# Projecting nodes for layer 1 of a four-layer graph attention stack while layer 0 still gathers

## The chip, the cores and the metric

The kernel runs on one core of one Trainium2 chip. The metric is device time in microseconds (us), the median of several executions. A profile of one execution is read beside it. The engines are called TensorE (PE in the profile, PEld for its weight loads), VectorE (DVE), ScalarE (ACT), GpSimd (POOL) and SyncE (SP). Transfers are issued by an engine's queue and moved by 16 DMA engines.

## The reference

There are 3327 nodes with 256 features and an adjacency matrix in which a node has some 32 neighbours, itself among them. Four attention layers follow one another. Each ends in a residual sum and a layer normalisation over the features.

```python
x = layernorm(x + gatv2(x, adj, ...))   # layer 0
x = layernorm(x + gat(x, adj, ...))     # layer 1
x = layernorm(x + linear_att(x, adj))   # layer 2
x = layernorm(x + two_gat_layers(x))    # layer 3, 4 heads, twice

# layer 0: score[i,j] = sum_c a[c] * leaky_relu(g_src[i,c] + g_tgt[j,c])
# layer 1: Wh = h @ W.T ; s1 = Wh @ a1 ; s2 = Wh @ a2
#          e = leaky_relu(s1[:,None] + s2[None,:]) ; masked by adj
#          out = softmax(e, axis=1) @ Wh
# layer 2: as layer 1 without leaky_relu, with a bias
# layer 3: as layer 1 with 4 heads of 64 features and elu, applied twice
```

In layer 0 the score doesn't split into a part of i and a part of j, so it is worked out only for the neighbours. In the other layers the exponential of the score does split, up to a maximum of two terms, and the sum over neighbours becomes a dense matrix product with the adjacency.

## The kernel before

The nodes lie in 26 tiles of 128 rows (the last has 127); h holds the current features of a tile in SBUF through all layers.

*Layer 0* (`sparse0`). The 26 tiles form three groups (`SETS = (5, 9, 12)`). For each tile VectorE extracts the list of neighbours from the adjacency, and nodes of a group are sorted by their number of neighbours. GpSimd then gathers the neighbours' rows from a table in DRAM, up to 8 neighbours of 128 nodes in one step (`parts`; each neighbour is one indirect transfer, L527). VectorE scores them (L546, L552), ScalarE scales rows by their weights (L633) and TensorE adds them up through an identity matrix (L636). The work is written out by step: gathers run four steps ahead (`LEAD`), and a table `due` says which other work is emitted at which step, through `at_step`. Eleven gather buffers (`TURNS`) rotate. When a group's last tile is done, its sums are scattered back to the nodes' order in DRAM (L671), read into h (`take`), and normed (`finish_sums`, `finish_root`, `finish`: L696 to L714). For the last group this comes after all gathers.

*Layers 1 to 3* (`layers`). The target nodes are cut into four blocks of 7, 7, 6 and 6 tiles. For a block, a loop over the 26 source tiles j loads the adjacency tile (`adjacent`; in layer 1 the int32 original, cast to bf16 and stored in DRAM for later layers), makes the edge weights (`weigh`, L1075, VectorE: the larger of the target's rate and the source's, times adjacency), and multiplies them with the source's projected features `feat[j]` (L1159 for one head, L1198 and L1206 for four). After the loop the block's sums are added to h, and a generator `prepare` norms the block and projects it for the next layer: per tile a transpose on TensorE (`turn`, L1104), a copy by ScalarE (L1107), the projection (L1011), and exponentials and scaling by ScalarE (L1018 to L1023). Generators wait in `pending`; `work_off` advances one by a step after each source tile, so that next layer's projection lies between this layer's products. The rates of a block (`rates_of`) are separate products of the transposed features with `w_src` (L1048), their exponential (L1053), a write of the row to DRAM (L1057) and a load that spreads it to all partitions (L1064), both issued by SyncE. For layer 1 all four blocks are prepared ahead of the loop, with weights loaded and their dot products formed at that place. In layer 3's first half, `finish_hidden` does the elu on a block and projects it for the second half, in stages that `staged` spaces by steps.

Where an engine is in a `manual_schedule`, its instructions keep the order of the program; otherwise the framework orders them. In layer 0 all but SyncE are manual; in layers 1 and 2 only TensorE; in layer 3 TensorE, VectorE and ScalarE.

Of the kernel before, what the change touches and what calls it, by code (L numbers as in the profile page):

```python
# [19 lines left out]
P = 128  # L20
# [26 lines left out]
def gat_stack(  # L47
# [55 lines left out]

    def copy_rows(engine, dst, src):

        rows = dst.shape[0]
        whole = rows // 16 * 16
        for lo, hi in ((0, whole), (whole, rows)):
            if lo < hi:
                engine.dma_start(dst[lo:hi], src[lo:hi])  # L110
# [7 lines left out]
    def load_row(work, src, name):  # L118

        size = src.shape[0]  # L120
        t = work.tile([P, size], F32, tag="row_" + name, name=name, bufs=1)
        nc.sync.dma_start(
            t, bass.AP(tensor=src.tensor, offset=src.offset, ap=[[0, P], [1, size]])
        )
        return t
# [124 lines left out]
    def sparse0(lost):  # L250
        GROUP, TURNS, LEAD = 8, 11, 4
        starts = [sum(SETS[:s]) for s in range(len(SETS))]
        with ExitStack() as s0:
# [21 lines left out]
            for c in range(kc):  # L275
                t = io0.tile([P, dim], F32, tag="hs", name="dots0")
# [230 lines left out]
            ]  # L507
            held = {}
# [4 lines left out]
            def gather(q):  # L513
# [11 lines left out]
                g = gath.tile([P, GROUP, ROW], F32, tag=f"g{q % TURNS}", name="g")  # L525
# [86 lines left out]
            def combine(s, t):  # L612
# [30 lines left out]
                for g, k0, m in groups[-1:] + groups[:-1]:  # L643
# [4 lines left out]
                    for k in reversed(range(0, m - 1, 2)):  # L648
# [38 lines left out]
            def finish_sums(s):  # L687

# [4 lines left out]
                for k, it in enumerate(block):  # L693
# [3 lines left out]
                    nc.vector.bn_aggr(mv[:pn, k, :], stats[:pn])  # L697
                rstd = small.tile([P, max(SETS)], F32, tag="rstd0", name="rstd0", bufs=2)
# [10 lines left out]
            def finish(s):  # L709
                mv, rstd = moments.pop(s)  # L710
                for k in range(SETS[s]):
# [5 lines left out]
                    )  # L717

# [25 lines left out]
            for q, key in ends.items():  # L744
                at_step(q + 4, add_input, *key)
                at_step(q + 6, between.append, lambda key=key: put_back(*key))
                if key[1] == SETS[key[0]] - 1:
# [3 lines left out]
                    at_step(q + 18, finish, key[0])  # L751
            for it in range(SETS[0]):
                write_list(0, it)
# [35 lines left out]
            assert not between  # L789

# [182 lines left out]
    def layers(rs):  # L973
# [16 lines left out]
        class Layer:  # L990


            def __init__(self, name, slot, nh, leaky, load, bias=None):
                self.slot, self.nh, self.leaky, self.bias = slot, nh, leaky, bias
                self.weight = work.tile([P, kc, dim + nh], F32, tag="weight", name=name + "w")
                row_src, row_dst = load(self.weight)
                dots(work, self.weight[:, :, dim : dim + nh], self.weight, row_dst, nh)
                if leaky:
                    self.w_src = work.tile([P, kc, nh], F32, tag="w_src", name="w_src")
                    dots(work, self.w_src, self.weight, row_src, nh)  # L1000
                    self.rate_d = dram.tile([heads, n], F32, name=f"rate_{slot}{nh}_d")
# [3 lines left out]
            def project(self, j, ht, banks):  # L1005
# [4 lines left out]
                for k in range(kc):  # L1010
                    nc.tensor.matmul(  # L1011
                        pacc[:pn, : dim + nh], ht[:, k, :pn], self.weight[:, k, :],
# [3 lines left out]
                if self.leaky:  # L1016
# [5 lines left out]
                    for lo in range(0, dim, width):  # L1022
# [3 lines left out]
                        )  # L1026
                else:
# [12 lines left out]
            def rates_of(self, b, ht, banks):  # L1040


                c0, c1 = cols_of(blocks[b])
                for lo in range(0, c1 - c0, BANK):
                    hi = min(lo + BANK, c1 - c0)
                    pr = misc(banks)
                    for k in range(kc):
                        nc.tensor.matmul(  # L1048
                            pr[: self.nh, : hi - lo], self.w_src[:, k, :], ht[:, k, lo:hi],
                            start=(k == 0), stop=(k == kc - 1),  # L1050
                        )
                    row = work.tile([heads, BANK], F32, tag="spread", name="rate_row", bufs=4)
                    nc.scalar.activation(  # L1053
                        row[: self.nh, : hi - lo], pr[: self.nh, : hi - lo], AF.Exp,
                        scale=1.0 - SLOPE,
                    )
                    nc.sync.dma_start(  # L1057
                        self.rate_d[: self.nh, c0 + lo : c0 + hi], row[: self.nh, : hi - lo]
                    )
# [4 lines left out]
                nc.sync.dma_start(  # L1064
# [31 lines left out]
        def turn(b, banks):  # L1096

            ht = turn_p.tile([P, kc, wide], F32, tag="ht", name="ht")
            for it in blocks[b]:
                pn = rows_of(it)  # L1100
                at0 = (it - blocks[b][0]) * P
                tp = misc(banks)
                for k in range(kc):
                    nc.tensor.transpose(  # L1104
                        tp[:, k * P : k * P + pn], h[it][:pn, k * P : (k + 1) * P], ident[:pn, :pn]
                    )
                nc.scalar.copy(  # L1107
                    ht[:, :, at0 : at0 + pn],
                    tp[:, : kc * P].rearrange("p (k i) -> p k i", k=kc)[:, :, :pn],
                )  # L1110
                yield ht, it

        def prepare(nxt, b, banks, normed=True):
# [3 lines left out]
            for ht, it in turn(b, banks):  # L1117
                at0 = (it - blocks[b][0]) * P
                yield
                nxt.project(it, ht[:, :, at0 : at0 + P], banks)  # L1120
                yield
            if nxt.leaky:
                nxt.rates_of(b, ht, banks)
# [19 lines left out]
        def one_head(layer, nxt, banks_next):  # L1143

            for b, block in enumerate(blocks):
                work_until(lambda: not layer.leaky or layer.rate[b] is not None)
                accs = [bank(s) for s in range(len(block))]
                for j in range(nt):
# [17 lines left out]
                    if j >= LATER:  # L1166
                        work_off()
                work_until(lambda: not pending)
                for s, it in enumerate(block):
# [6 lines left out]
                    )  # L1176
                pending.append(prepare(nxt, b, banks_next, normed=False))
# [325 lines left out]
```

The softmax here doesn't subtract the row's maximum and nothing guards it: scores larger than these inputs give would overflow.

## Time and profile before

The median of three executions is 3262.66 us (3262.03 to 3264.55). The profiled execution spans 3261.5 us. Busy time by engine over the span:

| engine | busy us | share |
|---|---|---|
| TensorE | 2224.4 | 68% |
| TensorE weight loads | 1218.1 | 37% |
| VectorE | 2318.1 | 71% |
| ScalarE | 741.5 | 23% |
| GpSimd | 1029.6 | 32% |

Where the stages lie in the span:

| stage | from, to (us) |
|---|---|
| layer 0, until the last tile's weights | 0 to 1523 |
| layer 1's first edge weight | 1593 |
| layer 1, end of blocks 0, 1, 2, 3 | 1706, 1793, 1868, 1943 |
| layer 2 | 1943 to 2228 |
| layer 3, first and second half | 2228 to 2747, 2747 to 3262 |

The shares of the whole span are means over stages with different limits: GpSimd is idle after layer 0, and TensorE is less than half busy in it. So a row of the span says little about what a change in one stage is worth, and the stages are read one by one. Busy time of TensorE is modelled at its ends.

### The profile page before, as it was taken

What the parts mean: (1) busy time and instruction counts of PE and PEld (TensorE: products, weight loads), DVE (VectorE), ACT (ScalarE), POOL (GpSimd) and SP (SyncE); (2) the same over time, 40 slices, a digit from 0 to 9 for tenths busy, and PEclk for the clock granted to TensorE, in tenths of its full rate; (3) what the DMA queues carried; (4) which work ended last, traced back from release to release, by engine and by line L of the source; (5) the groups of instructions that cost most, each with busy time, mean ns of one, the idle gap of its engine ahead of it and who ended that gap; (6) DMA issues with size and microseconds to landing.
All of it is one profiled execution on the core that took longest, in us unless ns stands there. A gap on an engine that the chain in (4) does not pass through costs nothing.

```text
span 3261.5 us, 44647 instructions
## 1 busy us (share of the span) xinstructions
PE 2224.4 (68%) x15644; PEld 1218.1 (37%) x15644; DVE 2318.1 (71%) x6589; ACT 741.5 (23%) x2002; POOL 1029.6 (32%) x1034
## 2 busy tenths in 40 slices
PE   3203332343441444343899999999999999999997
PEld 2101111121220221111478888774334444334342
DVE  6789999999975655554235642117888788899998
ACT  0003231342341343333334431110111110110110
POOL 0077657777767777774000000000000000000000
PEclk7556666666765776676699999999999999999998
DMA  7466536555435444443466753332212212212111
GB/s 216 137 141 180 169 100 150 173 157 155 112 86 109 124 111 113 113 113 91 125 199 199 201 161 93 100 99 72 63 44 68 61 46 65 63 49 57 56 47 48
DMA packets 176842, 364.21 MB, mean 112 GB/s; under 512 B 33746, under 2 KB 118964, under 8 KB 176610
## 3 DMA queue, kind: packets, MB, share of 16 engines
q1 hardware_dynamic: 96682, 183.56, 19.8%
q0 software_dynamic: 49632, 141.57, 16.9%
q10 hardware_dynamic: 30296, 36.15, 3.2%
q8 instruction: 126, 2.06, 0.3%
q14 instruction: 106, 0.87, 0.1%
HBM read 320.99 MB, written 43.58 MB: 112 GB/s over the span
## 4 chain that ended last, share of the span: by engine, by line
PE 46%; DVE 4%; DMA 2%; ACT 1%; issue 1%; DVEq 0%; SPq 0%; POOL 0%; ACTq 0%; POOLq 0%
PE acc L1198 17%; PE acc L1159 15%; PE acc L1206 8%; PE misc L1011 3%; DVE e L1075 3%; PE misc L1048 1%; DMA at_i<-in_adj_t_dram 1%; PE misc L1104 1%; DMA at<-at_d 1%; PE misc L1280 0%; PE misc L1241 0%; PE acc L636 0%; DVE stats L1355 0%; DVE h L1353 0%; ACT feat L1023 0%
## 5 line engine op out<-in xcount | busy, mean ns | idle before, releaser
L527 POOL DMA_INDIRECT g<-table_d,lst x923 | 912.6, 989 | 295.6 <-issue 268.8
L1075 DVE SCALAR_TENSOR_TENSOR e<-rate,feat,at 128x896 f32<-128x896 f32 (+4 forms) x832 | 843.1, 1078 | 67.7 <-PE acc L1206 58.4
L636 PE MATMUL acc<-g,ident 128*128 128x512 f32 (+1 forms) x934 | 454.7, 644 | 545.2 <-ACT g L633 512.7
L1198 PE MATMUL acc<-e,feat 128*32 128x384 f32 (+2 forms) x6656 | 722.8, 514 | 5.2 <-DVE e L1075 2.4
L225 POOL TENSOR_TENSOR rstds<-rstds,minus_half 128x7 f32<-128x7 f32 (+1 forms) x12 | 19.6, 1633 | 1671.7 <-DVE rstds L224 1671.7
L636 PEld LDWEIGHTS acc<-g,ident 128*128 128x128 f32 x934 | 193.3, 211 | 783.7 <-ACT g L633 561.6
L546 DVE TENSOR_TENSOR y<-g,both 128x1024 f32<-128x1024 f32 (+2 forms) x240 | 276.0, 1173 | 238.4 <-DMA g<-table_d,lst 223.5
L1206 PE MATMUL acc<-e,feat 128*32 128x384 f32 (+3 forms) x3328 | 397.5, 512 | 0.0
L1198 PEld LDWEIGHTS acc<-e,feat 128*32 128x32 f32 x6656 | 245.1, 109 | 381.8 <-issue 262.5
L633 ACT ACTIVATE g<-g,w 128x256 f32<-128x256 f32 x923 | 370.6, 494 | 0.0
L552 DVE SCALAR_TENSOR_TENSOR y<-y,both 128x256 f32<-128x256 f32 x923 | 324.5, 415 | 0.0
L1159 PE MATMUL acc<-feat,e 128*128 128x257 f32 (+2 forms) x1352 | 307.4, 381 | 0.6 <-DVE h L1173 0.6
L1159 PEld LDWEIGHTS acc<-feat,e 128*128 128x128 f32 (+2 forms) x1352 | 253.2, 190 | 39.7 <-issue 4.1
L1159 PE MATMUL acc<-feat,at 128*128 128x257 bf16 (+2 forms) x2028 | 240.9, 276 | 7.5 <-DMA at<-at_d 7.3
L466 PE MATMUL key_rows<-key_diag,ones 128*128 128x128 f32 x52 | 17.8, 440 | 314.5 <-DVE key_diag L465 259.5
L1159 PEld LDWEIGHTS <-at 128*128 128x128 bf16 (+2 forms) x2028 | 200.2, 100 | 43.9 <-DMA at<-at_d 8.0
L1075 DVE SCALAR_TENSOR_TENSOR e<-rate,feat,at_i 128x896 f32<-128x896 f32 (+2 forms) x104 | 112.2, 1081 | 143.1 <-DMA at_i<-in_adj_t_dram 109.8
L1206 PEld LDWEIGHTS acc<-e,feat 128*32 128x32 f32 (+1 forms) x3328 | 136.1, 110 | 164.2 <-issue 150.4
L421 DVE MAX8 cand<-num 128x8 f32<-128x64 uint16 x1352 | 178.9, 209 | 1.0
L542 ACT COPY both<-own_of 128x256 f32<-128x256 f32 x26 | 9.7, 374 | 602.1 <-DMA own_of<-own_d,lst 469.2
L466 PEld LDWEIGHTS key_rows<-key_diag,ones 128*128 128x128 f32 x52 | 12.1, 278 | 327.8 <-DVE key_diag L465 216.0
L1092 ACT CAST at<-at_i 128x896 bf16<-128x896 int32 (+2 forms) x104 | 92.0, 885 | 108.5 <-DMA at_i<-in_adj_t_dram 104.2
(158 smaller groups left out, 1707.5 us busy)
## 6 DMA issues: line engine op xcount, KB each, us to landing
at<-at_d SPq DMA_DIRECT2D x150, 224.0 KB
at_i<-in_adj_t_dram SPq DMA_DIRECT2D x50, 448.0 KB
adj_i<-in_adj_dram SPq DMA_DIRECT2D x25, 832.0 KB
adj_i<-in_adj_dram SPq DMA_DIRECT2D x25, 831.5 KB
g<-table_d,lst POOLq DMA_INDIRECT x923, 2.8
at<-at_d SPq DMA_DIRECT2D x75, 192.0 KB
at<-at_d SPq DMA_DIRECT2D x75, 191.8 KB
at_d<-at ACTq DMA_DIRECT2D x50, 224.0 KB
```

The costliest lines, as they stand in the source:

```text
L421: nc.vector.max(cand[:, lo // CHUNK + c, :], v[:, c * CHUNK : (c + 1) * CHUNK])
L527: nc.gpsimd.indirect_dma_start(out=g[:, k - k0, :], out_offset=None, in_=table_d[:, :], in_offset=bass.IndirectOffsetOnAxis(ap=entry["lst" ...
L546: nc.vector.tensor_tensor(y, rows, minus_src[:, None, :].to_broadcast([P, m, dim]), op=ALU.max)
L552: nc.vector.scalar_tensor_tensor(y, y, 1.0, a, op0=ALU.mult, op1=ALU.mult, accum_out=sc)
L633: nc.scalar.activation(rows, rows, AF.Copy, scale=w[:, k : k + 1])
L636: nc.tensor.matmul(dst, ident, rows, start=start, stop=stop)
L1011: nc.tensor.matmul(pacc[:pn, : dim + nh], ht[:, k, :pn], self.weight[:, k, :], start=(k == 0), stop=(k == kc - 1),)
L1075: nc.vector.scalar_tensor_tensor(e[:pn, : c1 - c0], self.rate[b][:pn, h_of, : c1 - c0], q, at[:pn, : c1 - c0], op0=ALU.max, op1=ALU.mult,)
L1092: nc.scalar.copy(at[:pn, :w], at_i[:pn, :w])
L1159: nc.tensor.matmul(accs[s][:pn, : dim + 1], a[:pj, s * P : s * P + pn], f[:pj, : dim + 1], start=(j == 0 and part == 0), stop=(j == nt - 1 ...
L1198: nc.tensor.matmul(accs[x][p][q : q + 32, : hi - lo], f[:pj, at0 : at0 + 32], es[at0 // hd][:pj, lo:hi], start=(j == 0), stop=(j == nt - 1),)
L1206: nc.tensor.matmul(accs[x][pairs][h_of * 32 : (h_of + 1) * 32, : hi - lo], f[:pj, dim + h_of : dim + h_of + 1].to_broadcast([pj, 32]), es[ ...
```

## The change

There are five parts.

1. The first two groups (14 tiles, the first two blocks of layer 1) are transposed and projected for layer 1 at steps of layer 0's last group (`turn_next`, `project_next`), in PSUM that the neighbour lists no longer use. The features go to DRAM (`feats_d`), and so do the rates (`rate1_d`). Layer 1's weights are loaded and their dots formed some steps earlier (`load_next`, `dots_next`) into a tile of their own, `w1`.
2. The last group's reading, moments and norms become a generator, `last_group`, that is worked off between the steps of layer 1's block 0, followed by the projection of the 12 tiles left. `fetch` brings the stored features three tiles ahead. In this block two generator steps are taken at each source tile from the eleventh on, and VectorE, ScalarE, GpSimd and SyncE keep program order.
3. Rates come from the projection: it has as many more columns as heads, their exponential is taken with the features', and each tile's rates are written to DRAM as single elements by ScalarE's queue. `rates_of` only loads them, also on ScalarE's queue. The separate products L1048 are gone, in all layers.
4. In `finish_hidden` elu and projection come at lags 6 and 7 in place of 4 and 5.
5. Smaller: the buffers that gathers rotate through are shifted so that the last ones lie at given places, the last tile's pairs are added in ascending order, layer 2's weights are loaded after layer 1's block 0, and transposed tiles have two small buffers in place of one for a whole block.

```diff
-                g = gath.tile([P, GROUP, ROW], F32, tag=f"g{q % TURNS}", name="g")
+                g = gath.tile([P, GROUP, ROW], F32, tag=f"g{(q + SHIFT) % TURNS}", name="g")
...
+            def turn_next(it):
+                bank = turned1["bank"]
+                for k in range(kc):
+                    nc.tensor.transpose(
+                        bank[:, k * P : (k + 1) * P], h[it][:, k * P : (k + 1) * P], ident
+                    )
+                ht = turned1[it] = io0.tile([P, kc, P], F32, tag="xt", name="ht1", bufs=4)
+                nc.scalar.copy(ht, bank[:, : kc * P].rearrange("p (k i) -> p k i", k=kc))
+
+            def project_next(it):
+                ht, p = turned1.pop(it), turned1["bank"][:, BANK : BANK + dim + 2]
+                project(p, ht, P, w1)
...
+                nc.sync.dma_start(feats_d[at0 : at0 + P, :], f[:, : dim + 2])
+                nc.sync.dma_start(
+                    rate1_d[:, at0 : at0 + P].rearrange("h p -> p h"), f[:, dim + 2 : dim + 3]
+                )
...
-                if key[1] == SETS[key[0]] - 1:
+                if key[1] == SETS[key[0]] - 1 and key[0] < len(SETS) - 1:
                     at_step(q + 10, take, key[0])
...
+            at = begins[len(SETS) - 1]
+            at_step(at - 6, load_next)
+            at_step(at - 3, dots_next, 0)
+            at_step(at - 2, dots_next, 1)
+            for s in range(len(SETS) - 1):
+                for it in range(starts[s], starts[s] + SETS[s]):
+                    at_step(at, turn_next, it)
+                    at_step(at + 2, project_next, it)
+                    at += 3
+                at = max(at, begins[len(SETS) - 1] + 19)
...
+            def last_group():
+                s = len(SETS) - 1
+                take(s)
+                for _ in range(4):
+                    yield
+                yield from settle(s)
+                finish_root(s)
+                yield
+                for lo in range(0, SETS[s], 6):
+                    finish(s, lo, lo + 6)
+                    yield
...
-                        pacc[:pn, : dim + nh], ht[:, k, :pn], self.weight[:, k, :],
+                        pacc[:pn, : dim + self.extra], ht[:, k, :pn], self.weight[:, k, :],
...
+                    rate = small.tile([P, heads], F32, tag="rate", name="rate_of")
+                    nc.scalar.activation(
+                        rate[:pn, :nh], pacc[:pn, dim + nh : dim + 2 * nh], AF.Exp,
+                        scale=1.0 - SLOPE,
+                    )
+                    copy_rows(
+                        nc.scalar,
+                        self.rate_d[:nh, j * P : j * P + pn].rearrange("h p -> p h"),
+                        rate[:pn, :nh],
+                    )
...
-                for lo in range(0, c1 - c0, BANK):
-                    hi = min(lo + BANK, c1 - c0)
-                    pr = misc(banks)
-                    for k in range(kc):
-                        nc.tensor.matmul(
-                            pr[: self.nh, : hi - lo], self.w_src[:, k, :], ht[:, k, lo:hi],
...
-                nc.sync.dma_start(
+                nc.scalar.dma_start(
                     rate[:, : self.nh, : c1 - c0], rows[None].to_broadcast([P, self.nh, c1 - c0])
                 )
...
-                    if j >= LATER:
+                    if layer is l1 and b == 0:
+                        work_off(2 if j > 10 else 1)
+                        fetch([j + 3])
+                        if j > early and late:
+                            l1.rates_of(late.pop(0))
+                    elif j >= LATER:
                         work_off()
                 work_until(lambda: not pending)
+                in_order.close()
...
-            yield from staged(units, [(0, spread), (3, scale), (4, elu), (5, project)])
-            l3b.rates_of(b, o, (6, 7))
+            yield from staged(units, [(0, spread), (3, scale), (6, elu), (7, project)])
+            yield
+            l3b.rates_of(b)
...
-        for b in range(len(blocks)):
-            pending.append(prepare(l1, b, (7,)))
-        work_until(lambda: l1.rate[0] is not None and not pending)
...
+        if early:
+            l1.rates_of(late.pop(0))
+        fetch(range(3))
+        if rest is not None:
+            pending.insert(0, rest)
```

## The prediction

> **What bounds the kernel now.** I read the 40 slices and the busy table of the page first, then the chain that ended last, then busy time by stage, then who waited for whom inside the stages that the change touches, and the timeline where one wait had to be understood.
>
> The table by stage (window, length, busy time and count of each engine, granted TensorE clock, DMA share, GB/s) cuts the span at events of the timeline: last combine of layer 0 at 1523, first layer 1 accumulation at 1598, end of layer 1's block 0 at 1706, end of layer 1 at 1945, layer 3 from 2228.
>
> ```profile
> 167.00:1523.00 1356.00, 498.17 (x1080) 232.45 (x1080) 1062.16 (x4434) 399.95 (x1024) 990.34 (x998) 0.67 0.49 131
> 1523.00:1598.00 75.00, 48.08 (x95) 21.11 (x96) 18.32 (x57) 23.11 (x69) 3.27 (x2) 0.59 0.27 82
> 1598.00:1706.00 108.00, 106.16 (x475) 82.79 (x475) 33.99 (x38) 46.32 (x102) 0.00 (x0) 0.99 0.64 190
> 1706.00:1945.00 239.00, 238.42 (x1120) 207.71 (x1119) 131.65 (x266) 93.62 (x174) 4.27 (x3) 1.00 0.67 194
> 1945.00:2228.00 283.00, 272.20 (x2219) 225.35 (x2217) 49.70 (x176) 43.38 (x176) 5.60 (x4) 0.98 0.35 99
> 2228.00:2747.00 519.00, 515.93 (x5340) 214.50 (x5341) 439.27 (x462) 64.31 (x226) 2.09 (x1) 1.00 0.21 57
> ```
>
> Layer 0 is paced by GpSimd: 923 gathers of 0.95 us with 0.30 us between them, while TensorE, VectorE and ScalarE have room. From 1598 on TensorE is busy nearly all the time. In between lie 75 us where no engine is full and the clock is at 0.59. The waits of 1545 to 1598 say why; the first lines are (who waited, on what: total, times, longest):
>
> ```profile
> DVE e L1075 <- DMA rate<-rate_f_d: 28.0, 1, 28.0
> ACT feat L1018 <- PE misc L1011: 27.7, 9, 10.4
> ...
> PE misc L1011 <- DMA l2w<-in_l_w_dram: 10.6, 1, 10.6
> ```
>
> and the timeline shows one tile's projection as a serial loop through one PSUM bank, 4.0 us from 1568.00 to 1572.00:
>
> ```profile
> 1568.00 0.69 PE L1104 MATMUL misc<-ident,h 128*128 128x128 f32 x2 [0.77 <-ACT feat L1023]
> 1568.72 0.37 ACT L1107 COPY ht<-misc 128x256 f32<-128x256 f32 x1 [0.78 <-PE misc L1104]
> 1569.15 2.08 PE L1011 MATMUL misc<-l1w,ht 128*128 128x257 f32 x4 [0.46 <-ACT ht L1107]
> 1571.27 0.17 ACT L1018 ACTIVATE feat<-misc 128x1 f32<-128x1 f32 x1 [2.17 <-PE misc L1011]
> ```
>
> So layer 1 starts late because weights, seven projections and the rates of block 0 stand in a row ahead of the first edge weight (1593). Block 0 then takes 108 us, as the other projections sit between its steps.
>
> Two smaller items. TensorE's waits in 2016 to 2228 and VectorE's in 2360 to 2880:
>
> ```profile
> PE acc L1159 <- DMA at<-at_d: 7.3, 3, 2.8
> PE misc L1048 <- ACT rate_row L1053: 2.0, 3, 0.7
> ```
>
> ```profile
> DVE o L1299 <- ACT spreads L1258: 42.6, 10, 5.5
> ```
>
> **What the skill says.** "DMA: Bandwidth & Descriptors", section "Queues, rings and completion order", says that each DMA engine goes round between the queues that have work, a packet at a time. The trace agrees with its other half: an adjacency load issued on SyncE at 2083.80, behind the 1792 KB rate load issued on the same queue at 2081.89, reached TensorE only at 2090.14. Its table of specifications says that pieces under 512 B are written by read-modify-write; no row here shows 4-byte pieces, which the change brings. "TensorE: Matmul & The Clock Gate", section "What's actually happening", has the clock halve after an idle window of some 3.4 us; here a 128x257 projection takes 2.08 us in 1545 to 1598 (clock 0.50) and 1.03 at 1619. "Perfetto Trace Analysis", section "Tensor Engine Instruction (MATMUL, LD_WEIGHTS)", calls the execution FIFOs of ScalarE, VectorE and GpSimd strict, unlike that of TensorE; so a ScalarE instruction that waits for TensorE holds all behind it, which the 42.6 us show.
>
> **The change part by part.**
>
> *Projection during layer 0.* 14 of 26 tiles get transposes and projection at one tile in three gather steps. A step is up to 8 gathers at 1.25 us, 10 us. A tile costs, at the slow clock, 0.69+2.08 us of TensorE and 0.37+3x0.17+0.47=1.35 us of ScalarE, in 30 us of which TensorE is busy 37% and ScalarE 29% (stage row). Weight dots add 8 VectorE operations of 0.4 us. GpSimd waited only 6.1 us in all for ScalarE to free a gathered buffer, so I cost this at nothing; it hides behind the gathers.
>
> *Start of block 0.* VectorE's order puts layer 0's last sum (L664, ends 1541.5) ahead of the first edge weight. The first adjacency tile may share memory with the last gathered rows: before, it was issued at 1540.51, its cast began at 1543.95; plus 1.15 us for L1075 gives 1545.1. Were it loaded earlier, 1542.6. I take 1545 for the start, against 1598.
>
> *Length of block 0.* 79 matmuls took 17.28 us at 1783, 0.219 each; 26 steps x 14 = 79.6 us. From the beats of block 1 (1736.20 to 1743.35 holds 28 matmuls, 6.12, and one tile), transposes and projection take 1.03 us on TensorE: 12 tiles, 12.4. In this block two generator steps run per accumulation step from step 11, so transposes and projection stand next to each other and TensorE waits for ScalarE's copy, 0.37 us plus two hand-overs, about 0.6: 12x0.6=7.2. The in-order ScalarE queue holds 13 reads of the last group's sums (1544.52 to 1554.2 before), which wait for the last scatter, ahead of the second adjacency cast. Behind them wait the casts, whose end frees buffers for the SyncE loads. Buffers are four steps deep, so a short stall: 0 to 8, taken 4. The norms of the last group need VectorE some 11 us (12 times 0.39+0.17, then the 3.96 us of L714) in eleven steps, where it is a third busy. Sum 103 us: block 0 ends at 1648 instead of 1706. Gain 58 (71 with no bubbles and the early start, 35 if block 0 runs on its transfers).
>
> *Rates from the projection.* The L1048 matmuls go; eight of the twelve groups lie after layer 1. In layer 2 they take 3.94, 3.94 and 3.52 us of TensorE's sequence (2074.97 to 2078.91 and so on), the fourth 2.90 busy and about 0.7 waiting: 15. In layer 3 their rows sum to 3.17+3.17+2.74+2.74=11.8. The projection widens from 260 to 264 columns, 1.5% of 1 us: nothing. Each tile gains a ScalarE exponential of 0.17 us and a transfer of 512 four-byte elements. Price from both sides: at the adjacency loads' 0.71 us of DMA for 128 rows (0.285 share of 20 us, 8 loads, at 2110) 512 pieces are 2.8 us; at the 10.5 ns per packet of the same DMA page (section "Bandwidth", measured table) an estimate of 5.4. They lie beside loads of 1.7 us a tile in a 5.2 us slot of layer 2, and only the far later rate load waits for them. With turns between queues I charge 3 us in all (0 to 36 if layer 2's loads starve).
>
> *Rate load on ScalarE's queue.* The adjacency load no longer stands behind it; of 7.3 us I take half, 3.6.
>
> *Later elu and projection in the hidden finish.* Before, at odd steps, ScalarE stood waiting for a projection while the exponentials of the next unit, needed by VectorE at once, queued behind. Now the elu comes three steps later. VectorE's 42.6 us is not TensorE's loss. Block 1 of that layer ran 136.1 us (2363.2 to 2499.3) where 26x4.51=117.3 plus finish rows 1.7+3.9+7.2+3.2=16.0 make 133.3; the four blocks lose 2.8, 3.9, 2.6 and 1.8. I take 10 of 11.
>
> Sum: 58+15-3+3.6+11.8+10=95. 3262.7-95=3167.
>
> **The rivals.**
> - *The wait moves into block 0.* It moves 26x672 KB of adjacency, 14x132 KB of features, 1.5 MB of sums and 0.9 MB of rates, 22 MB; at the 190 GB/s of the old block 0 that is 115 us, plus 11 of bubbles: gain 35. With half the later gains (18): 3210. For it: L1075 waited mostly on at_i in the old block. Against: 194 GB/s at 0.67 share shows room in the next blocks.
> - *Layer 0 gets longer.* If the early tiles' 14x4.1=58 us all stood in front of GpSimd's buffers: 3167+58=3225. Against: the 6.1 us.
> - *Slower.* Layer 2 starves by 36, layer 0 lengthens by 58, and in-order block 0 keeps its old length of 108 and stalls 20 more: start gain 53-20-58=-25, minus 36, plus 15 from the removed matmuls: 3309. It needs all three at once.
> - *All hidden*: 71+15+7+12+11=116: 3147.
>
> **How the numbers follow.** Forecast 0.75, block 0 on its transfers 0.14, longer layer 0 0.05, all hidden 0.03, slower 0.03. The range 3144 to 3212 takes in the all-hidden case and the transfer case. Faster 0.96, same 0.01, slower 0.03.
>
> **What would show it.** Right: the first layer 1 accumulation near 1545 and block 0's end near 1648; GpSimd's last gather still near 1515; no L1048 row; VectorE's wait for the spread exponentials near zero; no long wait for at after the rate loads. Wrong: DVE e waiting on at_i for more than 20 us in block 0, a last gather later than 1530, or TensorE waiting on at in layer 2 at each tile.

## The result and the profile after

The changed kernel takes 3309.57 us (median of four executions, 3302.12 to 3313.21), the kernel before in the same session 3263.11 (3262.03 to 3264.55). The ratio is 1.0139, 95% interval 1.0121 to 1.0157: slower by 46 us, where 95 us of gain were forecast.

The table by stage of the changed kernel, with the columns of the one shown of before (window, length, busy time and count of TensorE, its weight loads, VectorE, ScalarE, GpSimd; granted clock, DMA share, GB/s), is cut at the same events: the last gather, the first accumulation of layer 1, the end of its block 0, of layer 1, of layer 2, of layer 3's first half.

```profile
167.00:1532.00 1365.00, 526.07 (x1164) 248.56 (x1164) 1056.42 (x4412) 413.97 (x1094) 989.81 (x995) 0.67 0.55 131
1532.00:1569.00 37.00, 14.79 (x28) 6.45 (x28) 9.42 (x37) 12.22 (x30) 3.90 (x4) 0.68 0.26 73
1569.00:1710.00 141.00, 107.92 (x436) 88.49 (x436) 42.83 (x77) 35.85 (x84) 3.06 (x1) 0.88 0.85 162
1710.00:1951.00 241.00, 237.35 (x1101) 206.08 (x1102) 132.46 (x264) 97.92 (x179) 4.28 (x3) 0.99 0.71 204
1951.00:2305.00 354.00, 284.69 (x2181) 233.77 (x2180) 46.70 (x166) 41.56 (x190) 5.59 (x4) 0.91 0.52 78
2305.00:2801.00 496.00, 495.17 (x5289) 205.53 (x5291) 440.54 (x474) 61.33 (x240) 2.12 (x1) 1.00 0.39 60
```

Read the last two columns together. In layer 2 the DMA engines are busy 52% of the time and move 78 GB/s; before it was 35% and 99 GB/s. Block 0 of layer 1 shows 85% and 162 GB/s, before 64% and 190. More DMA time for fewer bytes per second means that packets take longer or are smaller and more; the experiments tell which. In layer 3's first half the share rises too, from 21% to 39%, but no wait comes of it there: the half is shorter, 496 us against 519.

The waits name who suffers. First TensorE's in layer 2 (2020 to 2250), then those of block 0 (1545 to 1700), then GpSimd's from 900 to 1540 (engine, line, on what: total, times, longest):

```profile
PE acc L1250 <- DMA at<-at_d: 47.2, 16, 6.8
```

```profile
DVE e L1168 <- DMA at_i<-in_adj_t_dram: 44.3, 9, 13.9
DVE e L1168 <- ACT feat L1119: 36.5, 6, 13.2
...
PE misc L1111 <- ACT turned L1198: 21.5, 12, 10.2
ACT at L1185 <- DMA at_d<-at: 21.1, 3, 12.6
...
PE acc L1250 <- DVE e L1168: 18.2, 4, 12.0
```

```profile
POOL g L538 <- issue: 127.1, 408, 1.7
POOL g L538 <- DMA g<-table_d,lst: 17.9, 23, 3.0
```

The prediction had set three signs against itself, and they have come, the third less often than it said: TensorE doesn't wait at each tile of layer 2. Its wait of 7.3 us for at there is now 47.2 us in this window, and 69.0 us in 22 waits over all 78 steps of the later three blocks (2018 to 2305). GpSimd waited 3.0 us for gathered rows in the same window of the kernel before; it waits 17.9 now, and the last gather starts at 1532 in place of 1515.

```profile
POOL g L527 <- DMA g<-table_d,lst: 3.0, 10, 0.3
```

The first sign is a poor one. In its old block 0 VectorE waited even longer for adjacency loads, while TensorE was busy 106 of 108 us (1598 to 1706):

```profile
DVE e L1075 <- DMA at_i<-in_adj_t_dram: 65.7, 24, 6.4
```

Now TensorE idles a quarter of block 0. Of the 18.2 us for edge weights, 12.0 lie ahead of its first product. The larger part, 21.5 us, is waiting for the copies of transposed tiles by ScalarE. They stand in ScalarE's order behind the casts of the adjacency, and a cast waits until an earlier one has been stored in DRAM (at_d):

```profile
1665.73 0.94 ACT L1185 CAST at<-at_i 128x896 bf16<-128x896 int32 x1 [12.57 <-DMA at_d<-at]
1667.10 0.37 ACT L1198 COPY turned<-misc 128x256 f32<-128x256 f32 x1 [0.43 <-ACT at L1185]
1667.52 2.09 PE L1111 MATMUL misc<-w,turned 128*128 128x258 f32 x4 [10.19 <-ACT turned L1198]
```

The timeline of layer 2 shows what stands ahead of a wait for at (an ACTq row is a transfer issued by ScalarE, and its second number is the issue alone):

```profile
2064.72 2.50 PE L1250 MATMUL acc<-feat,at 128*128 128x257 bf16 x21
...
2066.15 0.37 ACTq L116 DMA_DIRECT2D rate3a_d<-rate_of  x1
...
2072.44 0.37 ACTq L116 DMA_DIRECT2D rate3a_d<-rate_of  x1
2075.43 4.70 PE L1250 MATMUL acc<-feat,at 128*128 128x257 bf16 x21 [4.26 <-DMA at<-at_d]
```

The adjacency loads are on SyncE's queue; the writes of single elements are here on ScalarE's. In 2018 to 2305 such a write of 2 KB takes 11.3 us from issue to landing (median). The last row also shows a second cost of a wait: its 21 products take 4.70 us, where 21 took 2.50 us in the first row. The granted clock was 0.50 in 2075.4 to 2079.6 and 1.00 in 2064.7 to 2067.2.

Two parts of the change did what they were for: VectorE's wait for the spread exponentials (42.6 us) is gone, and the first accumulation of layer 1 comes at 1569 in place of 1599.

### The profile page after: what moved, and what is told of

It reads as the page before. It is cut to its first block, busy times and chain, and to the rows that moved or that the text cites. A ratio compares the mean times of both kernels' runs of the same rounds, so it can differ in the third digit from the quotient of the medians.

```text
span 3311.3 us, 44692 instructions
## 1 busy us (share of the span) xinstructions
PE 2210.2 (67%) x15548; PEld 1220.3 (37%) x15548; DVE 2313.8 (70%) x6589; ACT 735.8 (22%) x2056; POOL 1032.4 (31%) x1034
## 4 chain that ended last, share of the span: by engine, by line
PE 41%; DMA 8%; DVE 4%; issue 1%; ACT 0%; SPq 0%; POOL 0%; ACTq 0%; DVEq 0%; POOLq 0%
PE acc L1297 17%; PE acc L1250 13%; PE acc L1305 8%; DMA at<-at_d 4%; DVE e L1168 2%; PE misc L1111 2%; DMA at_i<-in_adj_t_dram 1%; DMA at_d<-at 1%; PE acc L647 0%; PE misc L1379 0%; DMA rate_d<-rate_of 0%; PE misc L1340 0%; PE misc L1195 0%; DVE stats L1455 0%; DVE h L1453 0%
## 5 line engine op out<-in xcount | busy, mean ns | idle before, releaser
L1297 PE MATMUL acc<-e,feat 128*32 128x384 f32 (+2 forms) x6656 | 689.5, 514 | 2.3 <-DVE e L1168 0.6
L1305 PE MATMUL acc<-e,feat 128*32 128x384 f32 (+3 forms) x3328 | 374.6, 512 | 0.0
L1297 PEld LDWEIGHTS acc<-e,feat 128*32 128x32 f32 x6656 | 231.9, 110 | 374.8 <-issue 281.7
L1250 PE MATMUL acc<-feat,e 128*128 128x257 f32 (+2 forms) x1352 | 315.4, 391 | 27.0 <-DVE e L1168 19.2
L1250 PE MATMUL acc<-feat,at 128*128 128x257 bf16 (+2 forms) x2028 | 260.8, 290 | 69.3 <-DMA at<-at_d 69.0
L1250 PEld LDWEIGHTS acc<-feat,e 128*128 128x128 f32 (+2 forms) x1352 | 263.0, 196 | 69.5 <-issue 19.4
L1250 PEld LDWEIGHTS <-at 128*128 128x128 bf16 (+2 forms) x2028 | 208.6, 105 | 117.7 <-DMA at<-at_d 76.6
L1305 PEld LDWEIGHTS acc<-e,feat 128*32 128x32 f32 (+1 forms) x3328 | 126.8, 110 | 165.4 <-issue 156.1
```

The costliest lines, as they stand in the source:

```text
L1250: nc.tensor.matmul(accs[s][:pn, : dim + 1], a[:pj, s * P : s * P + pn], f[:pj, : dim + 1], start=(j == 0 and part == 0), stop=(j == nt - 1 ...
L1297: nc.tensor.matmul(accs[x][p][q : q + 32, : hi - lo], f[:pj, at0 : at0 + 32], es[at0 // hd][:pj, lo:hi], start=(j == 0), stop=(j == nt - 1),)
L1305: nc.tensor.matmul(accs[x][pairs][h_of * 32 : (h_of + 1) * 32, : hi - lo], f[:pj, dim + h_of : dim + h_of + 1].to_broadcast([pj, 32]), es[ ...
```

## The experiments

Two theories stood against each other at first. Theory E: the writes of rates as 4-byte elements hold up all other transfers. Theory O: the new order of block 0, with other data behind one another in the queues, is the loss. Lengths below are read from the trace; a block ends at the first reciprocal (L1172 before), or in layer 3 at the first copy of its sums, after it. Where no range of times is given, there was one execution.

**Rates in rows, by tile.** Each tile's rates come from a small product of their own and go to DRAM as one row of 512 bytes per head.

```diff
-                        rate[:pn, :nh], pacc[:pn, dim + nh : dim + 2 * nh], AF.Exp,
+                        rate[:nh, :pn], pacc[:nh, BANK - P : BANK - P + pn], AF.Exp,
...
-                    copy_rows(
-                        nc.scalar,
-                        self.rate_d[:nh, j * P : j * P + pn].rearrange("h p -> p h"),
-                        rate[:pn, :nh],
-                    )
+                    nc.scalar.dma_start(self.rate_d[:nh, j * P : j * P + pn], rate[:nh, :pn])
```

> Theory E: the writes of rates as single 4-byte elements hold up every other transfer, gathers and adjacency loads among them. Here the changed kernel keeps all its parts, but the rates of a tile come from a small product of their own (w_src against the transposed tile, 2 to 4 more passes of 128 columns) and are written as one 512 B row for each head. E expects the last gather back near 1515 us (1532 in the changed kernel), TensorE's wait for at in layer 2 down from 69 to under 10 us, block 0 of layer 1 down from 141 to 100 to 115 us, and a time of 3165 to 3195. Rival O (order): the in-order queues of block 0 and the rate load and rate writes on ScalarE's queue cost the time, in whatever form the pieces are; it expects at least 3290, with the waits where they are.

Measured: 3210.65 us (3209.41 to 3211.56), ratio to before 0.9841 (0.9824 to 0.9857). The last gather is back at 1514.4, TensorE's wait for at is 8.3 us, and layer 2's later three blocks take 210.9 us in place of 286.8. The form of this write turns a loss of 46 us into a gain of 52, although the kernel now pays for more products than the changed one. That is far from O's 3290, but above E's range of 3165 to 3195 too: block 0 still takes 119 us from the first accumulation (1550.6 to 1669.7), where 103 were forecast and E allowed 115.

**Rows of ones.** The rates are worked out as in the changed kernel, but rows from a tile of ones are written in their place; so the rates' values are left out.

```diff
-                    copy_rows(
-                        nc.scalar,
-                        self.rate_d[:nh, j * P : j * P + pn].rearrange("h p -> p h"),
-                        rate[:pn, :nh],
-                    )
+                    nc.scalar.dma_start(self.rate_d[:nh, j * P : j * P + pn], same[:nh, :pn])
```

> The changed kernel with one edit: in place of each element write, a transfer of as many bytes on the same queue at the same place, as rows of 512 B from a tile of ones. So the rates that layers 1 and 3 use are all one: the values are left out, not the work. The products are those of the changed kernel. E expects within 15 us of the row version (3160 to 3190), O expects 3290 or more.

Measured: 3172.2 us, in E's range, though not within 15 us of the row version, which was slower than E had it. Block 0 takes 111.0 us, layer 2's later blocks 69.1, 60.9 and 60.7. As the ones depend on nothing, 20 of layer 3a's 26 writes ran in the first 170 us of the kernel and their loads didn't fall into layer 2: this run leaves the rates' traffic out of layer 2.

**The writes alone.** The kernel before, with one unread write of 512 elements for each tile in layer 3a's projections and nothing else.

```diff
+                    if self.slot == "f" and nh > 1:
+                        copy_rows(
+                            nc.scalar, extra_d[:nh, j * P : j * P + pn].rearrange("h p -> p h"),
+                            f[:pn, dim : dim + nh],
+                        )
```

> The kernel before with one thing added: for each of the 26 tiles projected for layer 3's first half, a write of 128x4 single elements of 4 B to a DRAM tile that nobody reads, on ScalarE's queue. E expects layer 2 to grow from 279 us by 50 to 90 us, with TensorE waiting for at by about that much, and the time to be 3310 to 3350. O expects under 10 us more, as nothing waits for these writes.

Measured: 3336.96 us, 74 more than before. Layer 2's later blocks take 97.8, 94.9 and 89.8 us in place of 73.0, 68.1 and 70.2; all other blocks keep their length within 3 us. Theory E stands: writes of 2 KB a tile, 20 of which fall into these three blocks, cost 71 us in a stage of 211, though nothing waits for them. Theory O doesn't explain the loss of 46 us; the order has a smaller share, which comes below. In a second execution, on another chip (below), TensorE's waits in 1990 to 2300 were:

```profile
PE acc L1166 <- DMA at<-at_d: 59.5, 21, 5.7
```

**Later elu and projection alone** (lags 6 and 7 in the kernel before).

```diff
-            yield from staged(units, [(0, spread), (3, scale), (4, elu), (5, project)])
+            yield from staged(units, [(0, spread), (3, scale), (6, elu), (7, project)])
```

> The kernel before with only the lags of the hidden finish at 6 and 7 in place of 4 and 5. My step forecast 10 us less (3253), with VectorE's wait for the spread exponentials in layer 3 falling from 42.6 us to near zero. Rival: TensorE paces these blocks anyway and the time stays within 3 us.

Measured: 3239.43 us (3238.14 to 3245.43), ratio 0.9927 (0.991 to 0.9943). VectorE's wait for the exponentials is gone, and the four blocks are 5.2, 6.2, 5.1 and 4.4 us shorter: 21, where 10 were forecast. The rival (within 3 us) falls.

**What makes an element write dear?** Four variants of the added write change where the pieces go; the first changes their size too.

```diff
-    extra_d = dram.tile([heads, n], F32)            # pieces of 4 bytes, side by side
+    extra_d = dram.tile([nt * P, heads], F32)       # 128 pieces of 16 bytes, side by side
+    extra_d = dram.tile([nt * P, heads, P], F32)    # 512 pieces of 4 bytes, 512 bytes apart
+    extra_d = dram.tile([heads, nt * P, 16], F32)   # 64 bytes apart
+    extra_d = dram.tile([heads, nt * P, 2], F32)    # 8 bytes apart
```

> The kernel before, with one unread write of a tile's four source terms in each of layer 3a's projections, as 128 pieces of 16 bytes that lie side by side, in place of 512 pieces of 4 bytes. Theory N (each piece holds the other transfers up by a like amount): a quarter of the 74 us that 512 pieces cost, 3281 (3272 to 3290). Rival Z (bytes count, not pieces): 3337 again, as it is the same 2 KB. Rival S (only pieces of 4 bytes are slow): 3263.

> The kernel before, with the same 512 pieces of 4 bytes for each tile, but every piece 512 bytes from the next. Theory N (each piece counts, wherever it goes): 3337 (3320 to 3350). Rival L (pieces that fall into one line of 512 bytes wait for each other's read and write back): most of the 74 us goes, 3265 to 3290.

These two fell to another chip, on which the kernel before takes 3687 us; in their traces layer 1 starts some 420 us later. So their times say little (3680.1 and 3689.1), and the stages have to be read. Layer 2's later blocks were 73.0, 66.5, 70.3 us and 73.0, 68.2, 71.9: no cost in either. Theory N, by which each piece counts, falls, and so does Z; S, by which the size of 4 bytes is enough, falls with the second. To be sure that this wasn't the chip, the dear write, the one 512 bytes apart and one 64 bytes apart ran on one chip.

> The kernel before with an unread write of 512 single elements, side by side in four rows, for each tile of layer 3a's projection, on the same chip as the two variants that follow. Every theory: layer 2's later blocks 90 to 98 us each in place of 68 to 73, 74 us over before.

> The same 512 pieces of 4 bytes, each 512 bytes from the next. Theory L (pieces that fall into one line of 512 bytes wait for each other): layer 2's later blocks stay at 66 to 73 us, as its first run showed on another chip. Rival C (that chip was another one, and the first run says nothing): 90 to 98 us.

> The same 512 pieces, each 64 bytes from the next, so that eight fall into one line of 512 bytes; if a DMA engine takes eight neighbouring rows, all eight come from one engine. Theory L1 (several engines that write into one line at once wait for each other): no cost, layer 2's later blocks 66 to 73 us. Theory L2 (any two pieces in one line, of one engine too): a cost, 75 us or more in at least one block.

Beside 3260.59 us for the kernel before they took 3330.46, 3257.33 and 3258.22; layer 2's later blocks were 95.0, 98.7, 90.6, then 73.0, 66.3, 70.2, then 73.0, 68.3, 70.7. So C and L2 fall. L1 isn't shown by that: under its own assumption of eight rows for an engine, four engines would meet in each 512 bytes of the 16-byte variant, which cost nothing. A last one closes the gap between 4 and 64 bytes:

> The kernel before with the same 512 unread pieces of 4 bytes for each tile, each 8 bytes from the next: eight fall into 64 bytes, 64 into 512. Theory G (pieces that fall into the same 64 bytes wait for each other, whoever writes them): a cost near that of pieces side by side, layer 2's later blocks 85 us or more each. Theory X (only pieces of different engines in the same 64 bytes do, and one engine takes eight neighbouring rows): no cost, 66 to 73 us. A cost in between would leave both open.

It took 3264.59 beside 3260.21 (3257.32 to 3261.82); layer 2's later blocks 74.3, 69.3 and 71.9 us. The packet view of layer 2's later blocks tells more than the time. Its columns are queue, packets, MB, and the time that its packets took as a share of 16 engines; q1 carries what SyncE issues, the adjacency loads above all, q10 the added writes. First the kernel before, then pieces side by side, 8 bytes apart, and 64 bytes apart:

```profile
q1 hardware_dynamic: 13050, 21.69, 35.8%
```

```profile
q1 hardware_dynamic: 13050, 21.69, 55.2%
q10 hardware_dynamic: 10560, 0.04, 2.1%
```

```profile
q1 hardware_dynamic: 13050, 21.69, 52.4%
q10 hardware_dynamic: 10560, 0.04, 2.7%
```

```profile
q1 hardware_dynamic: 13050, 21.69, 36.4%
q10 hardware_dynamic: 10560, 0.04, 2.5%
```

The same 13050 packets of SyncE's queue stand in each. Share times stage length gives their time:

| added pieces | stage, us | time of these packets, us of 16 engines |
|---|---|---|
| none | 211.3 | 75.6 |
| 512 of 4 bytes, side by side | 284.4 | 157.0 |
| 512 of 4 bytes, 8 bytes apart | 215.5 | 112.9 |
| 512 of 4 bytes, 64 bytes apart | 212.1 | 77.2 |

So the added writes' own packets cost next to nothing (2.1% of 284 us is 6 us for 20 writes, 0.3 each), but the loads' packets take twice as long in sum. Not each of them does: the median packet took 65 ns in all four traces, while one in a hundred took more than 0.49, 2.9, 2.0 and 0.48 us, in the order of the table. A few packets are held up for long. Eight bytes apart the sum is still half as long again, yet only some 4 us of it show in the time. Neither theory of the last run fits as it was put: G's 85 us a block falls, and X's "no cost" nearly holds for the time but not for the packets; the expectation had said that a cost in between leaves both open. Shown is that the hold-up belongs to pieces of 4 bytes that lie close together and is gone by 64 bytes. Whether closeness alone or several engines at one place make it was not settled.

**Rates turned by block.** The rates of a block stay in SBUF, a column for each head and tile; one transpose on TensorE turns them, one transfer writes rows of 512 bytes. No separate product for the rates is left.

```diff
+                    nc.scalar.activation(
+                        self.own.rearrange("p (h t) -> p h t", h=nh)[:pn, :, j - firsts[b]],
+                        pacc[:pn, dim + nh : dim + 2 * nh], AF.Exp, scale=1.0 - SLOPE,
+                    )
...
+                nc.tensor.transpose(self.rows, self.own, ident)
+                nc.scalar.copy(row[:m, :], self.rows)
+                nc.scalar.dma_start(self.rate_d[b][:m, :], row[:m, :])
```

> The changed kernel with the rates still taken from the projection, but kept in SBUF, a column for each tile and head, until a block is done; one transpose on TensorE turns them, and one transfer writes rows of 512 bytes. No product for the rates and no write of single elements. Theory E (the element writes are the whole loss): as the run with rows of ones: layer 2's later blocks about 61 us each, block 0 of layer 1 over at 1670, 3172 us (3160 to 3185). Rival T (a block's rates are now ready only at its end, and the trip through DRAM is waited for at the next block's start): the same block lengths, but gaps between blocks, more than 3195.

**Weights held back.** The same, and the loads and dot products of the weights of layers 2 and 3a are kept out of layer 1's block 0: the region of kept order ends after layer 2's weights, and layer 3a is set up after layer 2's block 0.

```diff
-                in_order.close()
...
                 if b == 0:
                     nxt = nxt()
+                in_order.close()
...
-        one_head(l2, lambda: l3a, (7,))
+        one_head(l2, third, (7,))
```

> As the run before, with the loads and dot products of the weights of layer 2 and of layer 3's first half held back to the end of layer 1's block 0 and to layer 2; of later weights only one load of 256 KB is left in block 0. Theory W (these loads and dot products, which stand between block 0's adjacency loads and edge weights, are what makes it 119 us in place of the 103 forecast): block 0 takes 105 to 112 us and the time is 7 to 14 us less. Rival B (block 0 waits for its transfers and for ScalarE's queue anyway): block 0 stays within 3 us of 119 and the time within 4 us.

The second edit also gives the weights of layer 3's second half a buffer of their own, and their load (256 KB) comes at the start of block 0. On the chip with the late layer 1 the first took 3602.36 and the second 3601.47 us beside 3686.97, with executions up to 20 us from the median, too wide to tell the two apart. But block 0 took 111.6 and 102.7 us from the first accumulation. They ran again on a chip where the kernel before took 3260.21:

> The changed kernel with rates turned and written by block as rows, on a chip where the kernel before takes near 3263: block 0 of layer 1 takes 111 us from its first accumulation, as on the other chip, and ends at 1665 to 1671; 3178 us (3170 to 3186).

> The same with the weights of layers 2 and 3 held back from block 0. Theory W: block 0 takes 103 us from its first accumulation, as on the other chip, and the time is 6 to 9 us below that of the run before; against the run whose last group's sums go through GpSimd's queue, no difference over 3 us, as that queue was not the limit. Rival B: the time within 3 us of the run before.

Measured: 3177.74 us (3176.54 to 3179.16), ratio 0.975 (0.9733 to 0.9766), and 3168.32 us (3167.11 to 3170.76), ratio 0.9719 (0.9703 to 0.9735). Block 0 took 112.3 and 103.4 us. The first is in theory E's range (3160 to 3185), so E stands and T falls. Its packets in layer 2's later blocks, beside those of the changed kernel, tie the loss to what the added writes showed: the same 11418 packets take 61.9 us of 16 engines (31.2% of 198.3) in place of 140.0 (48.8% of 286.8). The changed kernel first:

```profile
q1 hardware_dynamic: 11418, 16.41, 48.8%
```

```profile
q1 hardware_dynamic: 11418, 16.41, 31.2%
```

Theory W stands as well. Of the 8.9 us by which block 0 is shorter in the second, 5.2 are waits of TensorE for edge weights (5.4 to 0.2) and the rest shorter busy time (100.0 to 96.3). How the weights hurt is seen in VectorE's order in the run with the rates turned and the weights not held back (start, length, idle time before and its releaser in brackets):

```profile
1566.20 1.15 DVE L1194 SCALAR_TENSOR_TENSOR e<-rate,feat,at_i 128x896 f32<-128x896 f32 x1 [5.48 <-DMA at_i<-in_adj_t_dram]
1569.47 0.76 DVE L149 TENSOR_TENSOR dots<-l3aw,dst 128x256 f32<-128x256 f32 x2 [2.12 <-DMA dst<-in_l_a_dram]
...
1571.48 1.14 DVE L1194 SCALAR_TENSOR_TENSOR e<-rate,feat,at_i 128x896 f32<-128x896 f32 x1
```

and in SyncE's, where the loads for layer 3a stand between the adjacency loads:

```profile
1556.65 0.38 SPq L1509 DMA_DIRECT2D l3aw<-in_l_w_dram  x1
1559.57 0.38 SPq L1516 DMA_DIRECT2D src<-in_l_a_dram  x1
1560.32 1.27 SPq L120 DMA_DIRECT2D at_i<-in_adj_t_dram  x1
```

VectorE waits for a weight that TensorE first uses at 1996.7, more than 400 us later, and the edge weight behind it waits too. The program text has these loads after block 0; outside the region of kept order the framework had drawn them forward into it.

**The last group's sums through GpSimd's queue**, with the weights held back: the 13 reads of the sums leave ScalarE's queue.

```diff
-                    copy_rows(nc.scalar, h[it][:pn], sums_d[s][t * P : t * P + pn, :])
+                    copy_rows(engine, h[it][:pn], sums_d[s][t * P : t * P + pn, :])
...
-                take(s)
+                take(s, nc.gpsimd)
```

> The changed kernel with rates turned and written by block as rows, the weights of layers 2 and 3 held back from block 0, and the last group's sums read by GpSimd's queue in place of ScalarE's, where they stood ahead of the second adjacency cast. Theory Q (these 13 reads hold ScalarE's queue, and with it the casts, at the start of block 0): from the first accumulation to the end of block 0 95 to 100 us in place of the 103 of the run before; 3155 us in all on a chip where the kernel before takes 3263 (ratio 0.964 to 0.970). Rival B (block 0 is held by its transfers): 103 us again, 3160 or more.

Measured: 3170.05 us (3168.1 to 3174.68), ratio 0.9725 (0.9709 to 0.9741); block 0 took 102.8 us. Theory Q falls. The casts' wait for the sums is gone (9.9 us in 1500 to 1680 in the run before), and nothing is gained. Rival B's figure is met, but its reason, the transfers, isn't what the trace shows: TensorE is busy for 96 of the 103 us in both runs. In 1552 to 1664 of the run before its only long wait after the first product is the one for the copies of transposed tiles, 6.8 us in all.

## Why the prediction was wrong, step by step

**What bounds the kernel** was read rightly: the 75 us before block 0 could be used. **Start of block 0**: the first accumulation came at 1552.1 in the version with turned rates, and 1569.2 in the changed kernel, against 1545 forecast. The prediction took over the old issue of the first adjacency load at 1540.51. In the version with turned rates it is issued at 1545.18, behind the loads of the rates and of three tiles' features, and its cast begins at 1550.34 in place of 1543.95.

**The step that failed** is in "Rates from the projection": "With turns between queues I charge 3 us in all (0 to 36 if layer 2's loads starve)." Measured, it is 136 us: the changed kernel's profiled span of 3311.3 against 3175.0 with the same rates written in rows (132 by the medians). Between the events of the stage table the difference divides so:

| stage | changed, us | rates in rows by block, us | difference |
|---|---|---|---|
| to the last gather | 1532.2 | 1515.0 | 17.2 |
| last gather to the end of block 0 | 178.1 | 149.4 | 28.7 |
| rest of layer 1 | 240.4 | 238.7 | 1.7 |
| layer 2 | 354.5 | 266.1 | 88.4 |
| layer 3 | 1006.1 | 1005.8 | 0.3 |

In layer 2, 62 of the 88 us are longer waits for at (69.0 against 6.9), and 26 are slower products: TensorE is busy 285 us in place of 259 at a granted clock of 0.91 in place of 0.99. The stage of the version with rows, with the columns of the tables by stage:

```profile
1903.00:2169.00 266.00, 258.89 (x2190) 222.94 (x2189) 46.46 (x167) 42.31 (x193) 5.59 (x4) 0.99 0.37 104
```

The prediction priced the writes by their own packets, 2.8 to 5.4 us a tile, and let the queues take turns. Even that price was too high, as the added writes' packets took 0.3 us each; the cost lay in the loads beside them, for which the prediction had no term. The Trainium skill, "DMA: Bandwidth & Descriptors", section "Queues, rings and completion order", has the engines go round between queues packet by packet; that may be so, but the runs show that it doesn't protect the others, as the load packets themselves took longer in sum. The prediction had read in the same page's section "Specifications" that pieces under 512 bytes are read, changed and written back, and noted that no row of the trace showed 4-byte pieces: there the bound from above had to be open, not 36. The runs don't show how such pieces are written; they do show that size alone doesn't decide, since the same pieces 64 bytes apart cost nothing. The prediction also looked at layer 2 alone, while 14 of these writes (of 128 elements) lay among the gathers and 13 in block 0. The gathers follow each other at 1.25 us on GpSimd, whose waits for gathered rows rose from 3.0 to 17.9 us: 17 us came from 14 writes.

**Length of block 0**: 103 us forecast. It was 141 with element writes, 112.3 without, 103.4 with the weights also held back. The sum of its terms was right, and in the main the terms too: TensorE is busy 96.3 us (92.0 forecast) and waits 6.8 for the copies (7.2); the 4 us set aside for a stall came as busy time. But the prediction read the place of the weight loads from the program text, and the 9 us that they cost were not in it. The wait of VectorE in this block for ScalarE's features (47.6 us with the weights held back) costs nothing: TensorE waits only 0.2 us for edge weights there after its first product.

**Products removed**: 15 us in layer 2 and 11.8 in layer 3. The fourth group that the prediction counts in layer 2 runs at 2332.9, in layer 3's first block, so its terms are 11.4 and 15.4 when put where they belong. In layer 3 the version with turned rates is shorter than the one with the later lags alone by 4.0, 2.6, 2.6, 2.1 and 2.2 us in five blocks, 13.5 in all. Layer 2 is 12.9 shorter than before (279.0 to 266.1). Near in both.

**Rate load on ScalarE's queue**: 3.6 forecast, about nothing found. TensorE's wait for at in layer 2 is 6.9 us with turned rates, where it was 7.3. It is 0.5 us in the run with rows of ones, whose rate loads didn't fall into these blocks: the same megabytes hold the loads up from another queue.

**Later elu and projection**: 10 forecast, 21 by blocks and 24 by the medians. The length forecast for the second block, 133.3 us, was nearly met (134.3). But from end to end that block took 139.5 before, and the prediction set 136.1 against it, a window that began 3.2 us later.

**Early projection at nothing** was right by itself: with the rates in rows the last gather stands at 1515.0, where it was before, and GpSimd's wait for gathered rows, 2.1 us, isn't among its first four from 900 to 1540:

```profile
POOL g L542 <- issue: 128.4, 422, 0.3
POOL lists_d L501 <- DVE inv L674: 12.1, 1, 12.1
POOL sums_d L687 <- DVE hs L680: 4.3, 1, 4.3
POOL own_of L534 <- issue: 4.0, 13, 0.3
```

**The rival that ended at 3309** hit the time for wrong parts: it wanted layer 0 longer by 58, and it was 17; layer 2 to starve by 36, and it was 88; block 0 20 us over its old 108, and it was 33 over; and it left out layer 3, which became 33 us shorter. That the time came out is luck. It was given 3 in 100 because it "needs all three at once". They did come at once, since one cause stood behind them, wholly in layers 0 and 2 and for the most part in block 0. Chances of events with a common cause are not to be multiplied.

Without the element writes and the drawn-forward weights, the gain is 92 us (3260.21 to 3168.32), against 95 in the forecast's sum. That these are so near is in part luck. By stages of the profiles the gain up to the end of block 0 is 51 us (58 forecast), in the rest of layer 1 -3 (0), in layer 2 10 (16), and in layer 3 35 (22): the later elu gave more, the other parts less.

## What to carry to other kernels

Price a transfer by what it does to the transfers beside it, not by its own packets: compare DMA share and GB/s of a stage, and where the share rises while the rate falls, look for a write of many tiny pieces side by side. Keep values that lie across partitions in SBUF until there is a block of them, turn them once, and write rows. After a change of order, look in the trace at which loads really stand in a stage, and when several bad outcomes share a cause, give them one chance together.

## What the runs showed of the hardware that was not expected

- Twenty writes, each of 512 pieces of 4 bytes side by side in DRAM, 2 KB in all, doubled the time of 13050 packets on another queue (75.6 to 157.0 us of 16 engines), while their own packets took 0.3 us of the 16 engines a write. The median packet stayed at 65 ns; the slowest hundredth went from over 0.49 to over 2.9 us. The same pieces cost nothing 64 or 512 bytes apart, and neither did 128 pieces of 16 bytes side by side.
- One chip took 3687 us for the kernel that others ran in 3260 to 3263. In the traces of the first two variants, which ran there, the excess lay ahead of layer 1's first accumulation; from there on the blocks agreed with those of the kernel before, mostly to 0.2 us. Of GpSimd's idle time before gathers, 485 us were put down to issue on that chip (with the 16-byte pieces, up to 95 us at a time), and 269 for the kernel before elsewhere (up to 5 us). What causes it was not looked into.
